# A graph layer's front reordered, its values V split over two row halves, and its z products made of 64 rows

## The chip, the core and the metric

The kernel runs on one core of a Trainium2 chip. The metric is the device time of one execution in microseconds (us). The core has five engines that each work through their own instructions in program order: TensorE (PE, matmuls into PSUM), VectorE (DVE), ScalarE (ACT), GpSimd (POOL) and SyncE (SP, which here only issues DMAs).

## What is computed

`x` has 6,250 nodes of 128 channels; `src`, `dst` are 206,250 edges sorted by `dst`, self edges among them.

```python
h = jnp.maximum(_layernorm(x, axis=-1), 0.0)
feat = jnp.concatenate([h[dst], h[src] - h[dst]], axis=-1)
out = jax.ops.segment_max(feat @ W.T + b, dst, num_segments=6250)
return x + jnp.where(jnp.isfinite(out), out, 0.0)
```

A message is a part of `dst` plus a row B of `src` (B = h times the second half of W). So the kernel needs, for each node, the largest B row among its sources, and adds the part of the node itself at the end.

## The kernel before

**Names.** Nodes are numbered as 125 groups `l` of Q = 50 chunks `q` for B, and as 128 groups of LD = 49 destinations. Each of 128 partitions holds a window of 1,792 edges (`swin` sources, `dwin` destinations; L393, L394). B lies in SBUF as `Bp` (two fp32r parts, high and rest) and in DRAM as `Bt`.

**The front** (up to about 177 us). VectorE counts where each partition's window begins (L339, L388 to L391), and POOL gathers both windows. VectorE makes chunk numbers `q16` (L515 to L518), destinations clamped to their group `dlc` (L519, from `dlf`, which ScalarE writes at L516) and keys `KA`, `KB` (L520, L521). A loop of 44 compares of the keys with themselves shifted (L543 to L560) finds edges that repeat another's chunk and destination; TensorE sums the compares into the PSUM tile `dup` (`count`, L541), together with the masks `out_` (outside the group) and `selfm` (self edge, L561). Woven into this order by `ln_to` are 29 steps of the layernorm and of B: each scales on ScalarE (L454), turns (L460), splits into high and low parts (L462 to L468), multiplies (L477, L478) and copies out (L481 to L483, L494); every fifth one sends ten chunks to `Bt` and x plus the own part to `XA` (L487, L488, both issued by SP). `after` loads x in five groups of ten chunks, each load held back by a tiny copy. `moments`, `roots` and `scales` make the statistics. After the loop VectorE compacts the repeating edges (L571 to L606), POOL scatters them to DRAM (`Lt`, L607), SP reads them back (L612), and from the lists (L629 to L632) POOL begins 432 gathers of B rows (L77). `turned` transposes q16, dlc and the edges' worth into `TQ`, `TD`, `TV`. Some checks of the input stand last (L650 to L697).

**The main loop** (180 to 769 us). 13 tiles `t` of ten groups each (the last of eight) by 25 pairs `i` of chunks. For each pair, `one_hots` makes z in PSUM (L738: a selecting row of `Sel` times `Vb`) for each chunk of the **next** pair and ScalarE turns it into a one-hot by Relu (L739). TensorE multiplies B by the one-hots (L787, four products into `ps`), and VectorE takes the maximum with `acc2` (L798). Between these, `more_rows` issues the repeating edges' steps (L223, VectorE), 432 in all by pair 293, each group of eight stored to `M`. In tile 0, `self_edges` adds four products per pair; in tiles 1 and 2, ScalarE runs one `dump` (L810) per pair.

**V.** `Vb[t % 2]` holds for tile t an edge's source group per chunk and destination: v on rows 0 to 49, its square on rows 64 to 113, two rows of ones. It is built during tile t-1 by a written-out `plan`: `build` (four VectorE pieces per pair of groups), `mats` (14 products of 28 columns into the PSUM tile `pv`, L189, half of them at a time) and `values` (ScalarE). `values` reads `pv` four times (L198 square, L199 identity, for each of two l) and writes the squares shifted (L201): five instructions. It stands at pair 15 for three fifths of the tile, and at pair 23 for the rest. At pair 15 its instructions come ahead of the next half of `mats` (L715 to L720), which writes `pv`; `pv` has one buffer. In the text below a **burst** is one call of `values` in this loop.

**The end.** When the 432 steps have run (pair 293), POOL gathers 49 rows from `M` (L835), and VectorE joins them with `acc` and `XA` (L846 to L863).

Of the kernel before, what the change touches and what calls it, by code (L numbers as in the profile page):

```python
# [41 lines left out]
ONE = 50  # L42
SQ = 64
WN = 14
# [6 lines left out]
def gnn_kernel(tc, x, src, dst, W, b, out):  # L51
# [4 lines left out]
    assert C == P and Q * L == N and Q <= ONE and P * LD >= N and E >= WIN  # L56
# [5 lines left out]
    GQ = 10  # L62
    LASTD = N - (P - 1) * LD
# [16 lines left out]
    with ExitStack() as ctx:  # L80
# [9 lines left out]
        Sz = dram.tile([2 * Q - 1, P], F16, name="Sz")  # L90
        Sm = dram.tile([2 * Q - 1, P], F16, name="Sm")
# [9 lines left out]
        with ExitStack() as body:  # L101
# [5 lines left out]
            Sel = keep.tile([P, Q, P], F16, name="Sel")  # L107
# [40 lines left out]
            def build(u):  # L148

                o = (u % SLOTS) * SLOT  # L150
                OHQ = hx16[:, o:o + P * NBLK].rearrange("p (q b) -> p q b", b=NBLK)
                o += P * NBLK
                w = WN
                if u == NLP - 1:
                    o, w = SLOTS * SLOT, LD
                OHD = hx16[:, o:o + 2 * w * NBLK].rearrange("p (l w b) -> p l w b", w=w, b=NBLK)
                hots[u] = [OHQ, OHD]
                iw = IW if w == WN else IL

                def over(T, n):  # L160
                    return T[:, 2 * u:2 * u + 2].rearrange("p l (o b) -> p l o b", o=1).to_broadcast([P, 2, n, NBLK])

                def cmp_q(a, z):
                    iq = IQ[:, a:z].rearrange("p (o q) b -> p o q b", o=1).to_broadcast([P, 2, z - a, NBLK])
                    oh = at(OHQ, a * NBLK, [list(OHQ.ap[0]), [SQ * NBLK, 2], [NBLK, z - a], [1, NBLK]])
# [9 lines left out]
                return [cmp_d, mul_d, lambda: cmp_q(0, 25), lambda: cmp_q(25, Q)]  # L175
# [16 lines left out]
            def values(t, a, z):  # L192

                z = min(z, cols[t] // (2 * LD))
                pv, v, f = (m[:, :cols[t]].rearrange("q (p l d) -> q l p d", l=2, d=LD) for m in (pvs[t], Vb[t % 2], Vsq))
                for l in range(2):
                    r = slice(SQ * l, SQ * l + Q)
                    A_.activation(f[SQ:SQ + Q, l, a:z], pv[r, l, a:z], AF.Square, bias=shift_c[r, 1:2])  # L198
                    A_.activation(v[:Q, l, a:z], pv[r, l, a:z], AF.Identity, bias=shift_c[r, 0:1])  # L199
                w = slice(a * 2 * LD, z * 2 * LD)  # L200
                A_.activation(Vb[t % 2][SQ:SQ + Q, w], Vsq[SQ:SQ + Q, w], AF.Identity, bias=shift_c[SQ:SQ + Q, 2:3])  # L201

# [36 lines left out]
            with ExitStack() as pre:  # L239
# [64 lines left out]
                for i, v in enumerate((-0.5 * LD - 0.5, -0.25 * (LD * LD - 1), float(-L))):  # L304
                    G_.memset(shifts[:, i:i + 1], v)
# [10 lines left out]

                V.tensor_tensor(crow[:, 0], crow[:, 0], crow[:, 0], ALU.mult)
                V.tensor_scalar(crow[:, 0], crow[:, 0], -1.0, 1.0, op0=ALU.mult, op1=ALU.add)
                V.tensor_scalar(crow[:, 1], crow[:, 0], -2047.0, -2048.0, op0=ALU.is_lt, op1=ALU.mult)
                V.tensor_tensor(rows_[:, 3], crow[:, 0], crow[:, 1], ALU.subtract)  # L320
                V.tensor_copy(rows_[:, 2], crow[:, 1])
# [46 lines left out]
                brow = pool.tile([P, 2 * C], F32R, name="brow")  # L368
# [10 lines left out]
                for r in (0, 32):  # L379
                    V.memset(bsel[r:r + 1].bitcast(F32), 1.0)  # L380
                    A_.copy(brow[r:r + 1, C:], bsrc[r:r + 1])
                V.tensor_tensor(wlo, wT, whi.bitcast(F32), ALU.subtract)
                V.tensor_tensor(brow[32:33, C:], bsrc[32:33], brow[32:33, C:].bitcast(F32), ALU.subtract)
# [3 lines left out]
                after(V, blk_f[:1], GQ)  # L387
# [10 lines left out]


# [23 lines left out]
                for T, i in ((Sz, 0), (Sm, 1)):  # L423
                    for q0 in (0, Q):
                        nc.sync.dma_start(T[q0:q0 + Q - 1], zero[:Q - 1, :P].bitcast(F16))
                    nc.sync.dma_start(T[Q - 1:Q], rows_[:, i])
                nc.sync.dma_start(at(So, 0, [[2 * P, 1], [1, 2 * P]]), rows_[:, 2:4])

                for T, k0 in ((Sz, 0), (Sm, SQ)):
                    nc.sync.dma_start(selv[k0:k0 + Q], at(T, 0, [[P, Q], [1, Q * P]]))  # L430
                    nc.sync.dma_start(selv[k0 + Q:k0 + SQ], at(Sz, 0, [[0, SQ - Q], [0, Q], [1, P]]))
                nc.sync.dma_start(selv[ONE:ONE + 2], at(So, 0, [[P, 2], [0, Q], [1, P]]))
                nc.sync.dma_start(M_v[:, 0], none)

# [5 lines left out]
                V.memset(lw[96:], 0.0)  # L440
# [29 lines left out]
                def ln_mul(k):  # L470
                    st = steps[k]
                    st["pm"] = ps_m.tile([P, 2, 2 * C], F32, name="pm")
                    for j in range(2):
                        o = st["pm"][:L, j]
                        hi, lo = (slot(i, k)[:, j, :L] for i in (1, 2))
                        for a, w in ((bsel, brow), (hi, whi), (hi, wlo), (lo, whi), (lo, wlo)):
                            T_.matmul(o, a, w, start=j == 0 and a is bsel, stop=True, skip_group_check=True)  # L477
                    T_.matmul(st["pm"][:L, :, C:], ident[:L, :L], xs[:, 2 * k:2 * k + 2], start=False, stop=True,  # L478
                              skip_group_check=True)
# [28 lines left out]
                dlf = dwin.bitcast(F32)  # L508
                dlc = pool.tile([P, WIN], BF16, name="dlc")
                selfm = KB[:, :WIN].bitcast(BF16)  # L510
                v16 = lists[:, :WIN // 2].bitcast(BF16)
                q16 = pool.tile([P, WIN], BF16, name="q16")
                out_ = TV.rearrange("p s b -> p (s b)")
                ln_to(4)
                V.tensor_scalar(big, swin, (1 - Q) * 0.5, 1.0 / Q, op0=ALU.add, op1=ALU.mult)  # L515
                A_.activation(dlf, dwin, AF.Identity, bias=nthr)  # L516
                V.tensor_scalar(v16, big, MAGIC, -MAGIC, op0=ALU.add, op1=ALU.add)
                V.scalar_tensor_tensor(q16, v16, float(-Q), swin, op0=ALU.mult, op1=ALU.add)  # L518
                V.tensor_scalar(dlc, dlf, 0.0, float(LD + 1), op0=ALU.max, op1=ALU.min)  # L519
                V.scalar_tensor_tensor(KA[:, 64:], dlc, 64.0, q16, op0=ALU.mult, op1=ALU.add)  # L520
                V.tensor_copy(KB[:, 64:], KA[:, 63:63 + WIN])  # L521
                ln_to(6)

                A_.activation(out_, dlc, AF.Square, bias=shifts[:, 0:1])
                A_.activation(out_, out_, AF.Relu, bias=shifts[:, 1:2])
                A_.activation(big, swin, AF.Identity, bias=1.0)
# [16 lines left out]
                for s in range(1, POS + 1):  # L543
                    e = eqs[s % 3]
                    if s in (12, 24):
                        turned(*((q16, TQ) if s == 12 else (dlc, TD)))
# [6 lines left out]
                    count(identb, e, first=s == 1)  # L553
                    for g, s0 in ((2, 8), (3, 14), (4, 20)):
# [5 lines left out]
                    ln_to(6 + 9 * s // POS)  # L560
                V.scalar_tensor_tensor(selfm, dlf, nthr, swin, op0=ALU.subtract, op1=ALU.is_equal)  # L561
                count(nidb, out_)
                count(nidb, selfm, last=True)
# [16 lines left out]
                ln_to(ln_steps)  # L580
                where_i = pool.tile([P, 1], I32, name="where_i")
# [32 lines left out]

                val = q16
# [5 lines left out]
                for v in Vb:  # L621
                    G_.memset(v[96:], 0.0)
                    G_.memset(v[32:64], 1.0)

                for i in range(SLOTS):
                    for o in (Q, SQ + Q):
                        V.memset(hx16[:, i * SLOT + o * NBLK:i * SLOT + (o + SQ - Q) * NBLK], 0.0)
# [21 lines left out]
                same, junk = KA[:, :WIN].bitcast(BF16), KB[:, :WIN].bitcast(BF16)  # L649
                V.tensor_tensor(same[:, 1:], dlc[:, 1:], dlc[:, :WIN - 1], ALU.not_equal)  # L650
                V.tensor_tensor(same[:, 1:], same[:, 1:], selfm[:, :WIN - 1], ALU.mult)
                V.tensor_scalar(same[:, :1], dlc[:, WIN - 1:], float(LD), None, op0=ALU.is_le)
                V.tensor_tensor(same[:, :1], same[:, :1], selfm[:, WIN - 1:], ALU.mult)
                A_.activation(same, same, AF.Copy, accum_out=badc[:, 8:9])

                V.scalar_tensor_tensor(junk[:, 1:], dlf[:, 1:], 1.0, dlf[:, :WIN - 1], op0=ALU.mult, op1=ALU.is_lt,
# [35 lines left out]
                V.tensor_scalar(fl[:, 1:2], dlc[:, :1], 1.0, None, op0=ALU.is_lt)  # L692
                V.tensor_tensor(fl[:, :1], fl[:, :1], fl[:, 1:2], ALU.add)
# [4 lines left out]
            with ExitStack() as main:  # L698
# [33 lines left out]
                def one_hots(t, i):  # L732
                    n = cols[t]
                    both = []
                    for j in range(2):
                        z = ps_z.tile([P, 512], F32, name="z")
                        oh = ohp.tile([L + 1, TL * LD], F32R, name="oh")
                        T_.matmul(z[:, :n], Sel[:, Q - 1 - i - j], Vb[t % 2][:, :n], start=True, stop=True)  # L738
                        A_.activation(oh[:, :n], z[:L + 1, :n], AF.Relu)  # L739
                        both.append(oh)  # L740
                    return both
# [34 lines left out]
                for k, (t, i) in enumerate(pairs):  # L776
# [8 lines left out]
                    for j in range(2):  # L785
                        for e in range(2):
                            T_.matmul(ps[:, j, :n], Bp[:, e, i + j], oh[j][:, :n], start=e == 0, stop=e == 1)  # L787
# [151 lines left out]
```

## Time and profile before

| | us |
|---|---|
| median of 3 runs (811.27 to 813.49) | 811.47 |
| the profiled execution's own time | 809.35 |
| its span, first to last instruction | 807.6 |
| VectorE busy | 734.2 |
| TensorE busy | 662.4 |
| ScalarE busy | 511.8 |
| POOL busy | 502.5 |
| mean granted TensorE clock (share) | 0.942 |

The page gives busy time by engine, a strip of the span in 40 slices, DMA queues, the chain of work that ended last, and groups of instructions by line with the mean length of one and the idle time before them. A timeline lists instructions with start and length; in square brackets stands the idle time before one and what ended it. Matmuls overlap in the pipeline, so their distance in starts, not their length, is what one costs.

### The profile page before, as it was taken

What the parts mean: (1) busy time and instruction counts of PE and PEld (TensorE: products, weight loads), DVE (VectorE), ACT (ScalarE), POOL (GpSimd) and SP (SyncE); (2) the same over time, 40 slices, a digit from 0 to 9 for tenths busy, and PEclk for the clock granted to TensorE, in tenths of its full rate; (3) what the DMA queues carried; (4) which work ended last, traced back from release to release, by engine and by line L of the source; (5) the groups of instructions that cost most, each with busy time, mean ns of one, the idle gap of its engine ahead of it and who ended that gap; (6) DMA issues with size and microseconds to landing.
All of it is one profiled execution on the core that took longest, in us unless ns stands there. A gap on an engine that the chain in (4) does not pass through costs nothing.

```text
span 807.6 us, 12060 instructions
## 1 busy us (share of the span) xinstructions
PE 662.4 (82%) x3646; PEld 434.2 (54%) x3646; DVE 734.2 (91%) x1368; ACT 511.8 (63%) x1130; POOL 502.5 (62%) x538
## 2 busy tenths in 40 slices
PE   1688977259898998799989998989989999989950
PEld 0455766138765565455555555555555555556730
DVE  6698899888789899999999999999999999998972
ACT  2664487046789999667575766666576666657800
POOL 5200000377777777777777777777777777774773
PEclk9999999559999899799999999999999999999975
DMA  4631222312333333333333373333343333334152
GB/s 126 178 106 46 64 65 71 99 47 79 93 87 105 102 105 101 106 104 102 102 102 105 101 190 106 101 103 103 107 114 105 108 105 103 102 104 124 54 161 84
DMA packets 79650, 82.09 MB, mean 102 GB/s; under 512 B 11699, under 2 KB 68503, under 8 KB 79223
## 3 DMA queue, kind: packets, MB, share of 16 engines
q1 hardware_dynamic: 63038, 46.54, 20.4%
q0 software_dynamic: 15840, 33.93, 14.8%
q10 hardware_dynamic: 700, 0.78, 0.5%
q8 instruction: 30, 0.49, 0.2%
q14 instruction: 42, 0.34, 0.1%
HBM read 42.34 MB, written 38.82 MB: 100 GB/s over the span
## 4 chain that ended last, share of the span: by engine, by line
DVE 41%; PE 23%; issue 17%; ACT 10%; DMA 5%; POOL 2%; DVEq 0%; POOLq 0%; SPq 0%; ACTq 0%
DVE acc L798 16%; PE ps L787 10%; DVE rows L223 9%; ACT oh L739 4%; PE z L738 4%; PE dup L541 3%; DVE acc L593 3%; DMA rows<-Bt,lists 3%; PE pv L189 2%; DMA rows<-M,last_e 2%; ACT dump L810 2%; POOL rows L77 1%; ACT Vb L199 1%; ACT Vsq L198 1%; DVE acc L592 1%
## 5 line engine op out<-in xcount | busy, mean ns | idle before, releaser
L77 POOL DMA_INDIRECT rows<-Bt,lists x432 | 437.2, 1012 | 137.4 <-DMA rows<-Bt,lists 44.5
L739 ACT ACTIVATE oh<-z 126x490 fp32r<-126x490 f32 (+1 forms) x650 | 336.7, 574 | 156.7 <-PE z L738 149.6
L787 PE MATMUL ps<-oh,Bp 126*128 126x490 f32 (+1 forms) x1300 | 390.2, 423 | 23.4 <-DVE acc L798 16.2
L798 DVE TENSOR_TENSOR acc<-acc,ps 128x980 f32<-128x980 f32 (+1 forms) x312 | 359.2, 1151 | 23.4 <-PE ps L787 19.7
L787 PEld LDWEIGHTS ps<-oh,Bp 126*128 126x128 f32 x1300 | 235.3, 193 | 147.5 <-DVE acc L798 90.7
L738 PE MATMUL z<-Vb,Sel 128*128 128x490 f16 (+1 forms) x650 | 194.7, 378 | 14.7 <-ACT oh L739 8.8
L223 DVE SCALAR_TENSOR_TENSOR rows<-rows,lists 128x128 f32<-128x128 f32 x431 | 148.0, 343 | 1.4 <-DMA rows<-Bt,lists 0.4
L189 PEld LDWEIGHTS <-HX 128*128 128x128 bf16 x896 | 68.3, 159 | 52.7 <-issue 37.3
L189 PE MATMUL pv<-HX 128*128 128x28 bf16 (+1 forms) x826 | 74.0, 232 | 16.2 <-ACT Vb L199 16.2
L607 POOL DMA_INDIRECT Lt<-big,where_i x1 | 1.0, 1037 | 120.4 <-DVE big L606 120.4
L738 PEld LDWEIGHTS <-Sel 128*128 128x128 f16 x650 | 43.1, 104 | 55.5 <-issue 53.9
L166 DVE TENSOR_TENSOR HX<-T,IQ 128x700 bf16<-128x700 bf16 x128 | 65.5, 515 | 0.0
L77 POOL DMA_INDIRECT rows<-M,last_e x40 | 38.2, 956 | 12.2 <-issue 7.0
L541 PE MATMUL dup<-rows,identb 128*128 128x512 bf16 (+1 forms) x176 | 36.7, 352 | 4.4 <-DVE rows L552 3.9
L810 ACT ACTIVATE dump<-lists,nbias 128x512 bf16<-128x512 f32 x50 | 37.0, 741 | 0.1
L541 PEld LDWEIGHTS <-identb 128*128 128x128 bf16 x176 | 17.0, 97 | 21.2 <-issue 6.1
L552 DVE TENSOR_TENSOR rows<-KA,KB 128x1792 bf16<-128x1792 int16 x22 | 23.8, 1082 | 3.7 <-PE dup L541 3.7
L477 PE MATMUL pm<-whi,lhl 128*125 128x256 f32 x100 | 26.6, 287 | 0.0
L477 PE MATMUL pm<-wlo,lhl 128*125 128x256 f32 x100 | 26.5, 287 | 0.0
L552 DVE TENSOR_TENSOR rows<-KA 128x1792 bf16<-128x1792 int16 x21 | 22.8, 1085 | 1.4 <-PE dup L541 1.4
L454 ACT ACTIVATE rows<-HX,nmr,rstd 125x128 f32<-125x128 f32 x50 | 22.8, 525 | 1.1 <-DVE rows L440 1.1
L173 DVE TENSOR_TENSOR HX<-HX,T 128x392 bf16<-128x392 bf16 x64 | 23.2, 363 | 0.3
(239 smaller groups left out, 564.4 us busy)
## 6 DMA issues: line engine op xcount, KB each, us to landing
M<-rows SPq DMA_DIRECT2D x54, 512.0 KB
rows<-Bt,lists POOLq DMA_INDIRECT x432
HX<-in_x SPq DMA_DIRECT2D x5, 560.0 KB
Bt<-acc SPq DMA_DIRECT2D x5, 560.0 KB
XA<-HX SPq DMA_DIRECT2D x5, 560.0 KB
out_x<-rows SPq DMA_DIRECT2D x4, 448.0 KB
xa<-XA SPq DMA_DIRECT2D x1, 1512.0 KB
T<-XA SPq DMA_DIRECT2D x1, 1176.0 KB
```

What stands on the lines that cost most here:

```text
L77: G_.indirect_dma_start(out=o, out_offset=None, in_=table, in_offset=bass.IndirectOffsetOnAxis(ap=idx, axis=0))
L166: V.tensor_tensor(oh, over(TQ, z - a), iq, ALU.is_equal)
L189: T_.matmul(o2[:, :, lo:lo + w], OHQ[:, :, i], OHD[:, :, :, i], start=False, stop=True, skip_group_check=True)
L223: V.scalar_tensor_tensor(G[:, j], state["prev"], slim[:, k:k + 1], G[:, j], op0=ALU.min, op1=ALU.max)
L477: T_.matmul(o, a, w, start=j == 0 and a is bsel, stop=True, skip_group_check=True)
L541: T_.matmul(dup[:, c0:c1], m, e[:, c0:c1], start=first, stop=last)
L552: V.tensor_tensor(e, KA[:, 64:], i1, ALU.is_equal)
L738: T_.matmul(z[:, :n], Sel[:, Q - 1 - i - j], Vb[t % 2][:, :n], start=True, stop=True)
L739: A_.activation(oh[:, :n], z[:L + 1, :n], AF.Relu)
L787: T_.matmul(ps[:, j, :n], Bp[:, e, i + j], oh[j][:, :n], start=e == 0, stop=e == 1)
L798: V.tensor_tensor(a, a, ps[:, :, :n], ALU.max)
L810: A_.activation(dump, sdl, AF.Sign, scale=2.0, bias=nbias[:, c:c + 1], accum_out=ends[:, c:c + 1])
```

## The change

- **Clamp.** `dlf` and ScalarE's L516 go; `dlc` is made by two VectorE instructions from the integers. Keys use a factor 128.
- **Layernorm later.** Steps done before the loop and in it: 4 and 6 (before 6 and 9). x's second group is loaded after the window gathers like the others and its statistics move from ahead of the loop into it. `selfm` (now from bfloat16, against a shifted source `sl16` that ScalarE makes) and both mask counts move into the loop; `turned` of q16 and dlc moves behind the layernorm's last step.
- **XA.** One copy of x to XA, DRAM to DRAM, and per group an adding DMA that POOL issues; the product with x (L478) goes, and one of two products with the bias.
- **Checks.** The `same` part moves up to just behind the read of the lists; two tiny instructions go.
- **V** on four 32-row strips: chunks 0 to 24 on rows 0 to 24 with squares on 32 to 56, chunks 25 to 49 on rows 64 to 88 with squares on 96 to 120. `values` becomes ten instructions of the same columns. A pair is now chunk i/2 of each half; z comes from a product of 64 rows on rows 0 to 63 and one on 64 to 127. `Sel` halves.

```diff
                 for l in range(2):
-                    r = slice(SQ * l, SQ * l + Q)
-                    A_.activation(f[SQ:SQ + Q, l, a:z], pv[r, l, a:z], AF.Square, bias=shift_c[r, 1:2])
-                    A_.activation(v[:Q, l, a:z], pv[r, l, a:z], AF.Identity, bias=shift_c[r, 0:1])
+                    for h in range(2):
+                        r, o = (slice(o, o + H) for o in (SQ * l + SH * h, SQ * h))
+                        o2 = slice(SQ * h + SH, SQ * h + SH + H)
+                        A_.activation(f[o2, l, a:z], pv[r, l, a:z], AF.Square, bias=shift_c[r, 1:2])
+                        A_.activation(v[o, l, a:z], pv[r, l, a:z], AF.Identity, bias=shift_c[r, 0:1])
                 w = slice(a * 2 * LD, z * 2 * LD)
-                A_.activation(Vb[t % 2][SQ:SQ + Q, w], Vsq[SQ:SQ + Q, w], AF.Identity, bias=shift_c[SQ:SQ + Q, 2:3])
+                for o in (SH, SQ + SH):
+                    A_.activation(Vb[t % 2][o:o + H, w], Vsq[o:o + H, w], AF.Identity, bias=shift_c[o:o + H, 2:3])
...
-                after(V, blk_f[:1], GQ)
...
-                moments(GQ, 2 * GQ)
-                roots(GQ, 2 * GQ)
-                scales(GQ, 2 * GQ)
-                for q0 in range(2 * GQ, Q, GQ):
+                for q0 in range(GQ, Q, GQ):
                     after(G_, dwin, q0)
...
+                for l0, l1 in ((0, N // P * P), (N // P * P, N)):
+                    o, i = (a[l0:l1].rearrange("(p r) c -> p (r c)", p=min(P, l1 - l0)) for a in (XA, x))
+                    nc.sync.dma_start(o, i)
...
-                            nc.sync.dma_start(XA_l[p0:p1, q0:q0 + GQ], xs[p0:p1, q0:q0 + GQ])
+                            G_.dma_start(XA_l[p0:p1, q0:q0 + GQ], xs[p0:p1, q0:q0 + GQ], accum_op=ALU.add)
...
-                V.tensor_scalar(dlc, dlf, 0.0, float(LD + 1), op0=ALU.max, op1=ALU.min)
-                V.scalar_tensor_tensor(KA[:, 64:], dlc, 64.0, q16, op0=ALU.mult, op1=ALU.add)
+                V.tensor_scalar(dlc, dwin, nthr, 0.5, op0=ALU.add, op1=ALU.max)
+                V.tensor_scalar_min(dlc, dlc, LD + 0.5)
+                V.scalar_tensor_tensor(KA[:, 64:], dlc, 128.0, q16, op0=ALU.mult, op1=ALU.add)
...
+                    if s == 6:
+                        count(nidb, out_)
+                    if s == 9:
+                        V.tensor_tensor(selfm, dlc, sl16, ALU.is_equal)
+                        count(nidb, selfm)
-                    for g, s0 in ((2, 8), (3, 14), (4, 20)):
+                    for g, s0 in ((1, 1), (2, 9), (3, 17), (4, 25)):
...
-                    ln_to(6 + 9 * s // POS)
+                    ln_to(4 + 6 * s // POS)
...
-                        T_.matmul(z[:, :n], Sel[:, Q - 1 - i - j], Vb[t % 2][:, :n], start=True, stop=True)
+                        r = slice(SQ * j, SQ * (j + 1))
+                        T_.matmul(z[:, :n], Sel[r, H - 1 - i // 2], Vb[t % 2][r, :n], start=True, stop=True)
```

More of the change, by code (lines that the diff above doesn't have):

```diff
@@ L106, in gnn_kernel @@
             Bp = keep.tile([L + 1, 2, Q, C], F32R, name="Bp")
-            Sel = keep.tile([P, Q, P], F16, name="Sel")
+            Sel = keep.tile([P, H, P], F16, name="Sel")
             acc = keep.tile([P, Q * (L + 1)], F32, name="acc")
@@ L367, in gnn_kernel @@
                 bsel = pool.tile([P, L], F32R, name="bsel")
-                brow = pool.tile([P, 2 * C], F32R, name="brow")
+                brow = pool.tile([P, 2, C], F32R, name="brow")
                 whi = pool.tile([P, 2 * C], F32R, name="whi")
@@ L580, in gnn_kernel @@
                 ln_to(ln_steps)
+                turned(q16, TQ)
+                turned(dlc, TD)
                 where_i = pool.tile([P, 1], I32, name="where_i")
@@ L646, in gnn_kernel @@
                     f()
[L649 to L656, printed above, removed]
+                V.scalar_tensor_tensor(junk[:, 1:], dwin[:, 1:], 1.0, dwin[:, :WIN - 1], op0=ALU.mult, op1=ALU.is_lt,
                                        accum_out=badc[:, 0:1])
```

94 lines of the change are left out of this document (46 added, 48 removed).

## The prediction

> **What bounds the kernel now.** I read the strip of the page first, then busy time tile by tile, then waits in the main loop, then one burst of `values` in the timeline, then VectorE alone in the front.
>
> ```profile
> DVE  6698899888789899999999999999999999998972
> ...
> L798 DVE TENSOR_TENSOR acc<-acc,ps 128x980 f32<-128x980 f32 (+1 forms) x312 | 359.2, 1151 | 23.4 <-PE ps L787 19.7
> ...
> L738 PE MATMUL z<-Vb,Sel 128*128 128x490 f16 (+1 forms) x650 | 194.7, 378 | 14.7 <-ACT oh L739 8.8
> ```
>
> VectorE is full from the second slice almost to the end. By tile (start to start of a tile's first maximum; columns PE, PEld, DVE, ACT, POOL):
>
> ```profile
> 426.89:471.89 45.00, 41.83 (x224) 25.00 (x224) 44.85 (x85) 30.07 (x60) 34.64 (x35) 1.00 0.44 123
> ```
>
> This is tile 5: VectorE has 44.85 of 45.00 us, 1.80 per pair. It is the bound of tiles 3 to 10, and what TensorE saves there buys nothing by itself. TensorE's own need, from distances of starts (two z 0.43, four products 1.00, and 7 products of `mats` 0.42 twice in five pairs), is 1.60 per pair: 0.20 of slack. Where VectorE does wait, it waits once or twice a tile:
>
> ```profile
> DVE acc L798 <- PE ps L787: 19.7, 23, 3.2
> ...
> PE pv L189 <- ACT Vb L199: 16.2, 12, 2.1
> ```
>
> (Waits between 180 and 740 us: total, times, longest.) Twelve waits of TensorE for the last read of `pv`: one for each burst at pair 15. That of tile 5:
>
> ```profile
> 449.90 0.38 ACT L198 ACTIVATE Vsq<-pv,shift_c 50x147 f32<-50x147 f32 x1
> ...
> 450.29 0.38 ACT L199 ACTIVATE Vb<-pv,shift_c 50x147 f16<-50x147 f32 x1
> ...
> 450.69 0.38 ACT L198 ACTIVATE Vsq<-pv,shift_c 50x147 f32<-50x147 f32 x1
> ...
> 451.09 0.38 ACT L199 ACTIVATE Vb<-pv,shift_c 50x147 f16<-50x147 f32 x1
> 451.50 0.54 ACT L201 ACTIVATE Vb<-Vsq,shift_c 50x294 f16<-50x294 f32 x1
> 451.52 0.57 PE L189 MATMUL pv<-HX 128*128 128x28 bf16 x7 [0.98 <-ACT Vb L199]
> ...
> 451.93 0.58 PE L738 MATMUL z<-Vb,Sel 128*128 128x490 f16 x2
> 452.17 1.24 PE L787 MATMUL ps<-oh,Bp 126*128 126x490 f32 x4
> ...
> 453.44 1.18 DVE L798 TENSOR_TENSOR acc<-acc,ps 128x980 f32<-128x980 f32 x1
> ```
>
> Four reads, 0.40 apart; TensorE stands 0.98 until the last is done, then runs `mats`, z and the products that VectorE needs. They end at 453.40; VectorE had been free since 453.39. **The slack here is zero**, and in none of the twelve tiles is there more.
>
> The front, VectorE alone:
>
> ```profile
> 33.54 1.09 DVE L519 TENSOR_SCALAR dlc<-dwin 128x1792 bf16<-128x1792 f32 x1 [5.81 <-ACT dwin L516]
> ...
> 37.39 1.09 DVE L552 TENSOR_TENSOR rows<-KA,KB 128x1792 bf16<-128x1792 int16 x1
> ...
> 101.63 2.02 DVE L571 TENSOR_SCALAR KA<-dup 128x1792 bf16<-128x1792 f32 x1 [0.86 <-PE dup L541]
> ```
>
> It waits 5.81 for ScalarE's clamp; it is nearly full afterwards.
>
> **The front, step by step.**
> 1. *To the first compare.* Five small crow instructions and the copy at L268 leave the way to the window's begin: 0.5. x's second group (0.64 MB) no longer moves ahead of the window gathers (1.84 MB): the DMA ran at 330 GB/s there, so the gathers take 5.6 from about 16.7, plus 0.8 to the semaphore: dst at 23.1 (before 24.86), src about 20.3. From there VectorE runs L515, L517, L518 (1.13, 1.13, 2.05), the clamp (1.1, and 0.6 as L521), L520 2.05, L521 0.65: first compare at 29.0, not 37.39. **-8.4.**
> 2. *The loop.* It took 59.4: 44 compares at 1.00, three groups of moments at 3.1, and 5.85 of waits for TensorE. Now 44.1, four groups 12.4, selfm 1.05: 57.6. TensorE needs 44 x 0.75, 1.5 for the masks and 6 x 1.9: 46, so it no longer holds VectorE. The new moments wait for x's second group: its tiny POOL copies squeeze between VectorE's instructions (one took 2.00 beside L518), issue about 25.8, landed 3.4 later as the third group did: 29.2, needed at 30.0. If it is late, 1 to 2 us.
> 3. *After the loop.* L561 (2.06) and the wait of 0.86 before L571 are gone. L571 at 29.0 + 57.6 + 2.05 = 88.7, not 101.6: **-13.**
> 4. *Layernorm later.* 16 steps, not 11, stand before the product that VectorE needs at L596. A step took 3.01 there: 0.93 of ScalarE copies, 0.06, L492 0.22, ten products at 0.12, L478 0.63 to the release. With nine products and no L478 it would be 2.46; ScalarE's own work in it is 2.49. So 87.4 + 1.9 + 15 x 2.5 = 127; VectorE comes at 88.7 + 40.25 = 128.9. Hidden, by 2 us.
> 5. *Scatter and read back.* L606 ends at 135.4 (-12.9), but on POOL the last adding DMAs are queued ahead of the scatter; they wait for a copy at 134.7. No row shows an adding DMA. Bounds: issue as a gather (0.95 + 0.30 each; scatter at 137.3), or data at a tenth of the 330 GB/s (0.64 MB, 19 us, partly ahead of the scatter's own data). Nearest is the plain XA store of the same bytes, which lands in a few us: I take 3 lost. L629 at 145.5, not 154.96: -9.5 (-2 to -12).
> 6. *Checks* after L632 lose `same` and two small ones: 2.75, which run while VectorE waits for the lists. **Front: -12.2** (-5 to -15).
>
> ScalarE's extra instructions in the two first `values` (+4) end before the checks do (168.3 against 176.95, both moved): hidden.
>
> **The main loop.** VectorE's work is unchanged. The change adds five ScalarE instructions to each burst; their length goes with the columns (147, 98), not with the rows, so each costs the same again.
> - *Pair 15:* eight reads of `pv`, not four: TensorE waits 4 x 0.40 longer with nothing behind it that could run, and VectorE loses all of it: 12 x 1.6 = **+19.2**. The next one-hots come 2.1 later, still in time for the shifted pair 16.
> - *Pair 23:* five more cost 4 x 0.36 + 0.46 = 1.9. Queued behind them on ScalarE are the one-hots of pair 24, for which L787 waits (467.30 in tile 5). The products end at 468.53, VectorE comes at 469.56: slack 1.0 in tiles 3 to 6, 0.6 to 0.75 in 7 to 10, none in 0 to 2. So 4 x 0.9 + 4 x 1.25 + 3 x 1.9 = **+14.5**; that of tile 11 falls behind pair 293, where POOL's gathers from M bound the end.
> - *Tiles 1 and 2*, where ScalarE has 45.7 of 48.2, pay the whole 4.05 per tile: +1.
> - *z.* No product of 64 rows is in this trace. Floor: the two run at once, one of 0.215 saved per pair. Ceiling: they don't, and TensorE empties before and after: a z takes 0.378 but starts are 0.212 apart (tail 0.17, as much for the products after it), and the weight loads of 0.104 and 0.193 show: +0.6. Overlapped but emptied is +0.39. I take the middle of -0.215 and +0.39, +0.09, which lies under the slack of 0.20: 0 (-3 to +7, since the burst at pair 23 eats the same slack).
>
> The Trainium skill, TensorEngine Tiling (Array Packing), Key Properties, speaks on both sides: row tiles can work in parallel, and changing the tiling mode drains TensorE. No run here shows either; by the first alone z costs -0.2 per pair and the sum is the same, by the second it is the second rival.
>
> **Sum:** 809.35 - 12.2 + 19.2 + 14.5 + 1 = 831.9 against the profiled execution; the median shown is 2.1 above that one, so **834**. This case's own range: 822 to 848.
>
> **Rivals.**
> - *A faster kernel:* TensorE is what feeds the bursts, and with z nearly free it would have caught up enough for 1.6 and 1.9 to vanish. Then only the front counts: 811.5 - 12 = 799. For it: tile 0 is partly TensorE's. Against: at pair 15 TensorE stands still for ScalarE, and no speed of its own helps. It decides if the reads of `pv` in a burst take no longer than 1.7 us together.
> - *TensorE becomes the bound:* each pair goes from 128 rows to 64 and back. From a net +0.20 per pair on, every pair of tiles 1 to 11 pays: at +0.29, 0.09 x 275 = 25, tile 0 another 7, and the burst at pair 23 loses its slack (8 x 0.9 = 7): 873; at +0.39, 900. For it: two exposed weight loads and two tails are real durations. Against: at least one of the two z should overlap.
> - *The front gives nothing:* adding DMAs or a late x group eat the 12: 846.
> - *Half a burst:* bursts cost half of what I say, front at its best: 811, no change.
>
> **Chances.** Forecast 0.55, TensorE-bound 0.18, front lost 0.12, faster 0.12, half bursts 0.03. Leaving out the faster and half cases and the upper end of the TensorE-bound one: 812 to 880. 0.3% (2.4 us) is about what a measurement of this kernel can tell from none: faster 0.12, same 0.03, slower 0.85.
>
> **What would show it.** In the profile after: first L552-like compare near 29 us and lists near 145.5; the wait of `mats` for the last L199-like read about 2.6 in place of 0.98, with VectorE idle 1.6 before pair 15's maximum; tiles 4 to 6 near 47.5 us, not 45.1. I am wrong if the tiles keep 45, or if VectorE waits for TensorE in every pair.

## The result: slower, 880.7 us

The changed kernel takes 880.74 us in the median (875.22 to 884.45) beside 811.73 of the kernel before on the same chip: 1.084 times as long [1.079, 1.090]; such ratios and their intervals are taken from each kernel's fast executions alone. The forecast was 834, range 812 to 880. Slower was right, and the two mechanisms named are there, but the time is 47 us above the forecast and just outside the range.

In the page of the changed kernel (span 873.5 us) VectorE's row in the strip is no longer full, and in the group of its maxima (L800 now) the idle time ahead has gone from 23.4 to 95.9 us, while the busy time stands. The z products (L739 now) cost TensorE less, 140.9 in place of 194.7.

```profile
DVE  4999997786697977989888898878979888894883
...
PEclk9999997598798988989989899878989988996995
...
L800 DVE TENSOR_TENSOR acc<-acc,ps 128x980 f32<-128x980 f32 (+1 forms) x312 | 359.9, 1153 | 95.9 <-PE ps L789 94.6
...
L739 PE MATMUL z<-Vb,Sel 64*128 64x490 f16 (+1 forms) x650 | 140.9, 409 | 36.1 <-ACT Vb L205 23.3
```

Three sums locate the 65.9 us by which the span grew from 807.6. The first maximum comes at 170.62, not 180.07: -9.45. From there to the maximum of pair 293 (L800 in tile 11, pair 17; "the loop" below) it takes 625.5, not 550.3: **+75.3**. Behind it, +0.1. The loop stretch in busy time by window, first the kernel before, then the changed one (length, busy time of PE, PEld, DVE, ACT and POOL, mean granted TensorE clock, DMA share, GB/s):

```profile
180.07:730.32 550.25, 502.64 (x2683) 318.92 (x2683) 528.99 (x982) 391.42 (x825) 419.10 (x417) 0.97 0.38 105
```

```profile
170.62:796.14 625.52, 541.46 (x2684) 330.91 (x2683) 532.29 (x981) 435.48 (x940) 415.21 (x417) 0.88 0.35 92
```

VectorE's work is the same (529.0 and 532.3). ScalarE has 44 us more. The column to notice is the clock: 0.97 has become 0.88. The trace's record of the granted clock has 27.9 us at one half in the loop before and 148.1 after, in pieces of 3.4, 6.8 and 10.2 us, nearly all of them from pairs 14 and 23 on, which is where the bursts are (4.0 and 4.7 us of the two sums are the end of one long piece that began in the front). The burst at pair 15 of tile 5, in the timeline (columns: start, length, engine, line):

```profile
471.68 0.38 ACT L201 ACTIVATE Vsq<-pv,shift_c 25x147 f32<-25x147 f32 x1
...
474.43 0.38 ACT L202 ACTIVATE Vb<-pv,shift_c 25x147 f16<-25x147 f32 x1
...
474.83 1.10 ACT L205 ACTIVATE Vb<-Vsq,shift_c 25x294 f16<-25x294 f32 x2
474.86 0.56 PE L190 MATMUL pv<-HX 128*128 128x28 bf16 x7 [2.62 <-DVE HX L171]
...
475.35 0.38 PE L739 MATMUL z<-Vb,Sel 64*128 64x490 f16 x2
...
475.66 2.00 PE L789 MATMUL ps<-oh,Bp 126*128 126x490 f32 x4
...
477.69 1.17 DVE L800 TENSOR_TENSOR acc<-acc,ps 128x980 f32<-128x980 f32 x1 [2.60 <-PE ps L789]
```

Eight reads 0.39 apart; `mats` waits 2.62 for the last of them (the line names L171, which ended at 474.82, and the last read ended at 474.81; in eight of the twelve tiles the line names the read): the 0.98 of before plus 1.6, as forecast. The next line is the surprise: the four products take **2.00**, where they took 1.24 before. From 475.7 the clock is at one half for 3.4 us. VectorE waits 2.60 where the forecast had 1.6.

The burst at pair 23 of the same tile. Its Relus of pair 24 come behind it, z waits 1.98 for V and then for a buffer that those Relus free, the products run at half clock again, and VectorE waits 2.35:

```profile
489.56 0.34 ACT L201 ACTIVATE Vsq<-pv,shift_c 25x98 f32<-25x98 f32 x1
...
492.38 0.94 ACT L205 ACTIVATE Vb<-Vsq,shift_c 25x196 f16<-25x196 f32 x2
492.89 0.57 PE L739 MATMUL z<-Vb,Sel 64*128 64x490 f16 x1 [1.98 <-ACT Vb L205]
493.34 1.99 ACT L742 ACTIVATE oh<-z 126x490 fp32r<-126x490 f32 x4
493.97 0.57 PE L739 MATMUL z<-Vb,Sel 64*128 64x490 f16 x1 [0.51 <-ACT oh L742]
494.47 2.00 PE L789 MATMUL ps<-oh,Bp 126*128 126x490 f32 x4
...
496.51 1.17 DVE L800 TENSOR_TENSOR acc<-acc,ps 128x980 f32<-128x980 f32 x1 [2.35 <-PE ps L789]
```

All in all VectorE's waits ahead of the maxima of pairs 15 to 17 rose from 10.8 to 46.6 us in the loop, and of pairs 24, 0, 1 and 2 (the first three pairs of tile 0 left out) from 3.9 to 38.9: +70.8 of the 75.3. Pairs away from bursts are as before: the median step from one maximum to the next is the same at every pair from 6 to 14, 1.35 to 2.04 us.

### The profile page after: what moved, and what is told of

Read it like the earlier page. It is cut to its first block, busy times and chain, and to the rows that moved or that the text cites. A ratio compares the mean times of both kernels' runs of the same rounds, so it can differ in the third digit from the quotient of the medians.

```text
span 873.5 us, 12053 instructions
## 1 busy us (share of the span) xinstructions
PE 698.1 (80%) x3566; PEld 435.1 (50%) x3571; DVE 732.7 (84%) x1374; ACT 560.7 (64%) x1260; POOL 510.2 (58%) x548
## 4 chain that ended last, share of the span: by engine, by line
PE 35%; DVE 29%; ACT 13%; issue 13%; DMA 4%; POOL 1%; DVEq 0%; POOLq 0%; SPq 0%; ACTq 0%
PE ps L789 22%; DVE acc L800 10%; PE z L739 7%; DVE rows L227 6%; ACT oh L742 4%; PE pv L190 3%; ACT Vb L202 3%; ACT Vsq L201 3%; DVE rows L551 3%; DVE acc L596 3%; DMA rows<-Bt,lists 2%; ACT dump L812 1%; PE z L749 1%; DVE acc L595 1%; ACT Vb L205 1%
## 5 line engine op out<-in xcount | busy, mean ns | idle before, releaser
L742 ACT ACTIVATE oh<-z 126x490 fp32r<-126x490 f32 (+1 forms) x650 | 336.9, 575 | 185.6 <-PE z L739 184.4
L800 DVE TENSOR_TENSOR acc<-acc,ps 128x980 f32<-128x980 f32 (+1 forms) x312 | 359.9, 1153 | 95.9 <-PE ps L789 94.6
L789 PE MATMUL ps<-oh,Bp 126*128 126x490 f32 (+1 forms) x1300 | 413.7, 445 | 18.7 <-DVE acc L800 15.8
L789 PEld LDWEIGHTS ps<-oh,Bp 126*128 126x128 f32 x1300 | 245.3, 210 | 145.5 <-DVE acc L800 54.0
L739 PE MATMUL z<-Vb,Sel 64*128 64x490 f16 (+1 forms) x650 | 140.9, 409 | 36.1 <-ACT Vb L205 23.3
L739 PEld LDWEIGHTS <-Sel 64*128 64x128 f16 x650 | 32.6, 94 | 103.1 <-issue 94.0
L490 POOL DMA_DIRECT2D XA<-HX x10 | 9.8, 1212 | 96.4 <-ACT lhl L472 75.9
L78 POOL DMA_INDIRECT rows<-M,last_e x40 | 38.4, 959 | 12.2 <-issue 7.9
L78 POOL DMA_INDIRECT HX<-M,last_e x9 | 8.5, 944 | 50.2 <-DMA M<-rows 47.8
L202 ACT ACTIVATE Vb<-pv,shift_c 25x147 f16<-25x147 f32 (+2 forms) x96 | 34.1, 355 | 1.8
L201 ACT ACTIVATE Vsq<-pv,shift_c 25x147 f32<-25x147 f32 (+2 forms) x96 | 34.0, 354 | 1.3
L496 ACT CAST Bp<-pm 125x256 fp32r<-125x256 f32 x25 | 9.7, 387 | 35.1 <-PE pm L494 35.1
L205 ACT ACTIVATE Vb<-Vsq,shift_c 25x294 f16<-25x294 f32 (+2 forms) x52 | 25.6, 493 | 1.3
```

Of the source, the lines that this page charges most:

```text
L78: G_.indirect_dma_start(out=o, out_offset=None, in_=table, in_offset=bass.IndirectOffsetOnAxis(ap=idx, axis=0))
L201: A_.activation(f[o2, l, a:z], pv[r, l, a:z], AF.Square, bias=shift_c[r, 1:2])
L202: A_.activation(v[o, l, a:z], pv[r, l, a:z], AF.Identity, bias=shift_c[r, 0:1])
L739: T_.matmul(z[:, :n], Sel[r, H - 1 - i // 2], Vb[t % 2][r, :n], start=True, stop=True)
L789: T_.matmul(ps[:, j, :n], Bp[:, e, i // 2 + H * j], oh[j][:, :n], start=e == 0, stop=e == 1)
L800: V.tensor_tensor(a, a, ps[:, :, :n], ALU.max)
```

## The experiments

Theory A: a burst is longer than what one pair leaves free on ScalarE, TensorE and VectorE wait for it, and TensorE then runs on at half its clock. C: the length alone, at an unchanged clock (the forecast). B: 64-row products among 128-row ones cost the time. D, in one run: ScalarE's added work in all.

All times with the kernel before on the same chip at 812 to 813 us. "15" and "24": VectorE's waits before the maxima of pairs 15 to 17, and of 24, 0, 1, 2 (without the first three pairs of tile 0), in the loop; "half": the loop's time at half clock. The last four columns are of one execution each, the profiled one. In half bursts the ratio is of five of its ten executions, whose median is 821.4.

| kernel | median us | against before | loop | 15 | 24 | half |
|---|---|---|---|---|---|---|
| before | 811.7 | | 550.3 | 10.8 | 3.9 | 27.9 |
| changed | 880.7 | 1.084 [1.079, 1.090] | 625.5 | 46.6 | 38.9 | 148.1 |
| front only | 803.3 | 0.988 [0.984, 0.992] | 554.3 | 12.8 | 1.9 | 25.7 |
| values twice, 128 rows | 862.5 | 1.060 [1.056, 1.064] | 605.2 | 45.0 | 24.5 | 99.6 |
| half bursts, 64 rows | 825.9 | 1.008 [1.005, 1.011] | 572.9 | 20.3 | 6.4 | 84.3 |
| changed, filled | 839.7 | 1.035 [1.032, 1.038] | 583.2 | 28.9 | 19.1 | 5.0 |
| changed, bursts cut | 836.0 | 1.030 [1.026, 1.034] | 582.7 | 11.2 | 30.1 | 87.0 |
| changed, first burst moved | 897.7 | 1.106 [1.102, 1.110] | 643.5 | 1.6 | 53.2 | 182.5 |
| front only, bursts cut | 802.8 | 0.987 [0.984, 0.990] | 552.1 | 0.7 | 3.6 | 15.1 |

The table leaves out eleven runs, on chips where the kernel before itself took 1124 to 1137 us in the median (1092 to 1161 in single executions) and engines waited up to 29 us at a time for something that the trace does not name; they stand at the end of this section.

**Front only.** The diff of the front, with `values`, `one_hots` and the selector loads of before.

> The front of the changed kernel with V and z of the kernel before. All theories: 802 us (800 to 804) where the kernel before takes 811.7, by the first maximum that falls 9.45 us earlier. Against the run that also cuts the bursts (802.8): the same within 1.5 us if the stream of gathers sets the pace as soon as the bursts stop doing so, over 805 if cutting them had been worth the 10 us expected of it.

803.26 us, as expected: the front is worth 9.3 us (6.7 to 12.7 by the interval). In the profiled execution the first maximum comes 9.4 earlier, but the loop is 4.1 longer than before (554.3). POOL's gathers, which must be through before the maximum of pair 293, begin 7.0 earlier (150.4, before 157.4) and end only 5.7 earlier (721.5, before 727.2).

**Values twice**, in the kernel before:

```
                 for l in range(2):
                     r = slice(SQ * l, SQ * l + Q)
-                    A_.activation(f[SQ:SQ + Q, l, a:z], pv[r, l, a:z], AF.Square, bias=shift_c[r, 1:2])
+                    for _ in range(2):
+                        A_.activation(f[SQ:SQ + Q, l, a:z], pv[r, l, a:z], AF.Square, bias=shift_c[r, 1:2])
...
```

(and the same for the two other instructions, whose lines are left out here.)

> The kernel before with every instruction of values issued twice (the same results written again): 128-row products throughout, bursts of ten instructions in place of five. Theory A/C (burst length): 811.7 plus nearly all of the 75 us that the main loop lost, 877 to 887 us. Rival B (64-row products among 128-row ones cost it): 812.

862.48. Rival B's 812 is out: bursts of ten instructions cost 50 us without one 64-row product. But theory A's 877 is missed too: 20 us of the loop's 75 are not there, 14 of them at pairs 24 to 2.

**Half bursts**, in the changed kernel: `for h in range(1)` and `for o in (SH,)` in `values`, so that rows 64 to 127 of V are never written and the output lacks the values of chunks 25 to 49.

> The changed kernel without the second half of V (never written, so the output lacks the values of chunks 25 to 49): 64-row products as changed, bursts of five instructions. Theory A/C: 802 to 808 us. Rival B: over 865.

825.94: neither. Bursts of five at 64 rows take away most of the loss, yet 19 us more of loop than front only has is left. In the profiled execution 14 of them lie in tile 0, here by window (half bursts, then front only): 67.19 in place of 53.21, with a mean clock of 0.73. The first burst is followed by one piece of half clock of 34.1 us there. The ten executions spread more than those of the other kernels of the table, 814 to 834 us, and the longer ones have the lower mean clock (0.93 down to 0.89).

```profile
171.13:238.32 67.19, 65.13 (x323) 49.50 (x322) 46.61 (x81) 40.26 (x87) 50.33 (x54) 0.73 0.30 84
```

```profile
170.70:223.91 53.21, 49.74 (x326) 42.25 (x326) 45.91 (x81) 39.46 (x88) 40.44 (x42) 0.98 0.33 92
```

**Filled**, in the changed kernel:

```
+                    fill = i // 2 in (15, 24)
+                    if fill:
+                        ps = ps_s.tile([P, 2, 512], F32, name="ps")
+                        for _ in range(8):
+                            T_.matmul(ps[:, 0], Bp[:, 0, 0], Bp[:, 0, 0:4], start=True, stop=True)
                     for f in plan.get((t, i // 2), ()):
                         f()
...
```

> The changed kernel with eight more 512-column products on TensorE at pairs 15 and 24, ahead of the one-hot products; bursts as they are; the results of the added products are overwritten. Theory A (the halved clock behind each burst is what the forecast left out, some 40 us): 835 to 850 us. Theory C (the length of the bursts on ScalarE is all of it, the halved clock only goes with it): 870 to 890 us, though the half clock goes from behind the bursts.

839.74 us, in theory A's range, and the run that decides: 64-row products and bursts as they were, more work on TensorE, and 41 us less. The loop has 5.0 us at half clock in place of 148.1, and the clock column says 1.00:

```profile
172.32:755.56 583.24, 536.43 (x2868) 336.28 (x2867) 529.25 (x981) 435.36 (x940) 416.34 (x417) 1.00 0.36 99
```

The same burst of tile 5 in its timeline (L787 are the added products, L795 the pair's own, L806 the maxima):

```profile
455.36 2.11 PE L787 MATMUL ps<-Bp 126*128 126x512 f32 x8 [0.63 <-DVE acc L806]
...
457.33 1.10 ACT L205 ACTIVATE Vb<-Vsq,shift_c 25x294 f16<-25x294 f32 x2
457.36 0.58 PE L190 MATMUL pv<-HX 128*128 128x28 bf16 x7
...
458.18 1.15 PE L795 MATMUL ps<-oh,Bp 126*128 126x490 f32 x4
...
459.37 1.18 DVE L806 TENSOR_TENSOR acc<-acc,ps 128x980 f32<-128x980 f32 x1 [1.79 <-PE ps L795]
```

The burst takes as long as before; the products behind it take 1.15, not 2.00, and VectorE waits 1.79, not 2.60. What is left is what the forecast had: +33.0 in the loop (forecast 34.7), +18.0 at pairs 15 to 17 (19.2), +15.1 at pairs 24 to 2 (15.5 with tiles 1 and 2). The fit is closer than the comparison can bear: the kernel before, from which these are counted, has 27.9 us of half clock itself, and the added products take time too.

**Bursts cut.** `values` gets as arguments which of the two l to do and whether to write the squares, and is called in pieces of at most six instructions; the second half of `mats` for the tile's last pair of groups comes one pair earlier.

```
-                    at_pair(t, 5 * r + 2, lambda u=u: mats(u, NBLK // 2, NBLK, (ps_v, "pv")))
+                    at_pair(t, 5 * r + 2 - (r == PL - 1), lambda u=u: mats(u, NBLK // 2, NBLK, (ps_v, "pv")))
                     if r == 2:
-                        at_pair(t, 15, lambda t=t: values(t + 1, 0, 3))
+                        for i, how in ((13, ((0,), False)), (14, ((1,), False)), (16, ((), True))):
+                            at_pair(t, i, lambda t=t, how=how: values(t + 1, 0, 3, *how))
                     if u == NLP - 1 or r == PL - 1:
-                        at_pair(t, 5 * r + 3, lambda t=t: values(t + 1, 3, PL))
+                        for i, how in ((0, ((0,), False)), (1, ((1,), True))):
+                            at_pair(t, 5 * r + 3 - (r == PL - 1) + i, lambda t=t, how=how: values(t + 1, 3, PL, *how))
```

> The changed kernel, its halves of V and 64-row products kept, but each burst of values cut into pieces of four reads or fewer in different pairs (13, 14 and 16 in place of 15; 22 and 23 in place of 23, with the last one-hot products one pair earlier). Theory A/C (a burst stalls because it is longer than what one pair leaves free on ScalarE): the 75 us that the main loop lost come back nearly whole, 800 to 815 us where the kernel before takes 811.7, and the interval to pair 15's maximum falls from 4.3 to 4.9 us to 2.3 or less. Rival B (64-row products among 128-row ones): 865 and more, intervals as in the changed kernel. Rival D (ScalarE's added work in all, about 96 us of a main loop of 590, is what the loop pays): 860 and more, the idle time only moved to other pairs.

835.96. Rival D is out: ScalarE's added work is all still there (435.7 us busy in the loop, as in the changed kernel's 435.5), and 43 of the loop's 75 us are back. Not "nearly whole": the first burst, in pieces of four, costs no more than before the change (11.2 against 10.8), but the second, whose last piece has six, still stalls pair 24 (30.1), with a piece of half clock of 6.8 us behind it in most tiles.

**First burst moved**, whole, `values(t + 1, 0, 3)` from pair 15 to 18, behind the products of `mats` ("one-hot products" in the expectation) of pairs 15 and 17.

> The changed kernel with its first burst (ten instructions, uncut) moved from pair 15 to pair 18, behind the one-hot products of pairs 15 and 17, so that these no longer wait for it. If the loss at pair 15 needs the one-hot products queued behind the burst: the stall of pair 15 goes and none comes at pair 18, 840 to 850 us. If the burst's length on ScalarE is enough by itself (it delays the two Relus behind it): the stall of 2.6 us comes back at pair 19, 870 to 885 us.

897.70, above both ranges: the stall goes from pair 15 (1.6 us left) and comes at pairs 18 to 20 (47.0; in the changed kernel 1.0), no smaller, and half clock grows to 182.5 us. In tile 5, in the timeline (L739 z, L742 its Relu):

```profile
487.07 0.38 ACT L201 ACTIVATE Vsq<-pv,shift_c 25x147 f32<-25x147 f32 x1
...
490.23 1.10 ACT L205 ACTIVATE Vb<-Vsq,shift_c 25x294 f16<-25x294 f32 x2
...
491.35 1.99 ACT L742 ACTIVATE oh<-z 126x490 fp32r<-126x490 f32 x4
491.99 0.56 PE L739 MATMUL z<-Vb,Sel 64*128 64x490 f16 x1 [3.05 <-ACT oh L742]
...
492.48 2.00 PE L789 MATMUL ps<-oh,Bp 126*128 126x490 f32 x4
...
494.52 1.17 DVE L800 TENSOR_TENSOR acc<-acc,ps 128x980 f32<-128x980 f32 x1 [3.02 <-PE ps L789]
```

No product of `mats` waits here. The Relus stand behind the burst in ScalarE's order, the next z needs a buffer that they free, and VectorE waits 3.02, with the products at 2.00 once more. So the length of the burst is enough by itself; it is not the wait for `pv` in particular.

**Front only, bursts cut**: the best of both, since a burst of five at 128 rows also stalled pair 15.

> The front of the changed kernel, V and z of the kernel before, and the bursts of values cut over several pairs as in the run that cuts them in the changed kernel. Where the kernel before takes 811.7: 802 from the front alone, less the 10.9 us that VectorE waits at pairs 15 to 17 and part of the 3.9 at pairs 24 to 2: 790 to 800 us. If bursts of five instructions cost nothing that cutting recovers: 802.

802.78, 1.3% below the kernel before, but not below front only (803.26, on another chip): the 790 to 800 hoped for were missed, and the 802 of the expectation's other branch came for a reason that it does not name. The waits at pair 15 are gone, 0.7 in place of 12.8. In their place stands another (waits of 180 to 740 us: total, times, longest):

```profile
DVE rows L224 <- DMA rows<-Bt,lists: 12.4, 21, 1.9
```

That was 0.4, once, before (4.2 in front only). VectorE's stream step now waits for POOL's gathers: 432 of them at 1.0 us each with 0.3 between run from the lists on almost without a gap, and the last one ends at 721.0. In front only (721.5) and in the kernel before (727.2) they run just as densely, with one gap of over 1 us each, so the gathers set the pace as soon as the bursts do not, and cutting bursts has little left to win.

**Runs on disturbed chips.** Front only, values twice, half bursts and filled were first tried there, in this order:

> The change's front with the V, the z products of 128 rows and the five-instruction bursts of before. If the front gained what the two traces show between them at the first maximum (180.07 against 170.62), 811.7 - 9.5 = 802 us, and tiles 4 to 6 at 45 us each. If instead the new front disturbs the main loop (adding DMAs, gathers that begin earlier), tiles of 47 us or more and a time above 811.

> The kernel before with every instruction of values issued twice (the second writes the same values again): V, z of 128 rows and the front stay. Theory A (the length of a burst, and the halved clock that TensorE gets after standing still for it): nearly the whole loss of the main loop, 811.7 + 65 to 75 = 877 to 887 us, VectorE idle 2.5 to 3 before the maximum of pair 15. Theory C (the length of a burst at an unchanged clock, my forecast's sizes): 811.7 + 35 = 846, idle 1.6. Theory B (the change between 64 and 128 rows costs TensorE): no change, 812.

> The changed kernel with the second half of V never written (rows 64 to 127 keep the 1.0 of their memset), so that a burst is five instructions again; the z products of 64 rows stay. Chunks 25 to 49 give wrong one-hots, the instructions that follow are the same. Theories A and C: the loop is that of before, 802 us, up to 808 where the products of 64 rows use up slack. Theory B: above 865, tiles still 50 us or more.

> The changed kernel with eight filler products of 126 rows and 512 columns (overwritten by the real ones) ahead of the plan's work of pairs 15 and 24 of every tile, so that TensorE is not idle while ScalarE works off a burst. Theory A: the clock stays at 1.0 through the bursts, and VectorE's idle falls to the 1.6 and about 1 per tile of the lengths alone: 835 to 850 us. Theories B and C: nothing to win from activity, 875 to 890.

1130.6, 1141.0, 1142.6 and 1157.5 us, beside 1137.2 of the kernel before: no theory's numbers. Again, on another chip:

> The front of the changed kernel with V and z of the kernel before. Its first maximum falls 9.45 us earlier in the trace of the changed kernel; nothing behind it is touched. All theories: 811.7 - 9.45 = 802 us (800 to 804), and no more half clock than before (24 us). If it is at 811, what the front gains is given back at the end.

> The kernel before, with every instruction of values issued twice (the same results are written again): 128-row products throughout, eight reads and two spreads for each part of a tile instead of four and one. Theory A (a longer burst makes TensorE stand still for the one-hots, and it then runs at half clock): 811.7 plus most of the 75 us that the main loop lost, 877 to 887 us, with over 100 us at half clock. Rival C (longer bursts at an unchanged clock, as forecast): 846. Rival B (the change between 64-row and 128-row products): 812.

> The changed kernel without the second half of V (it is never written, so the output lacks the values of chunks 25 to 49): bursts of four reads and one spread, as before the change; 64-row products as changed. Theories A and C (burst length): 802 to 808 us, half clock back to some 25 us. Rival B (64-row products among 128-row ones): over 865.

> The changed kernel with eight more 512-column products on TensorE at pairs 15 and 24, ahead of the one-hot products, so that it has work while it waits for the values' burst; the bursts stay as they are, and the results of the added products are overwritten. Theory A (the halved clock is what the forecast left out): most of the 136 us at half clock goes, 835 to 850 us. Rivals B and C (the clock follows something else): 875 to 890, since the added products take some 1 us each time.

1120.9, 1143.9, 1127.3 and 1141.1 us, beside 1124.5. And front only on a third:

> The front of the changed kernel with V and z of the kernel before. Its first maximum falls 9.45 us earlier in the trace of the changed kernel, and nothing behind it is touched. All theories: 811.7 - 9.45 = 802 us (800 to 804), and no more half clock than before (24 us). If it is at 811, what the front gains is given back at the end.

1142.9 us, beside 1127.4. Nothing can be said from these sums. Two details of the traces agree with the later runs: front only's first maximum at 170.4, 170.2 and 171.0 us; and half clock in the 9 us from the first read of a burst, summed over the 24 bursts, 118 and 116 us with values twice and 51 and 34 in the filled runs. Over the whole loop, though, half clock is about as long in both there (343 and 345 us, 336 and 328). Two last runs, bursts cut and filled, and values twice and filled, were to settle whether the 20 us between the changed kernel and values twice are the clock's:

> The changed kernel with its bursts cut over several pairs and added products on TensorE (four at pair 15, six at pair 24) that keep its clock up; the results of the added products are overwritten. With both causes gone, only the 64-row products are left of the change behind the front. If they cost the loop only through the clock: the loop to pair 293's maximum takes some 570 us (552 of the run that cuts the bursts at 128 rows, and some 15 of waiting that is left at pair 24), 815 to 824 us in all. If they cost by themselves, 830 or more.

> The kernel before with every instruction of values issued twice and eight added products on TensorE at pairs 15 and 24 (their results are overwritten): the bursts of the change at 128 rows and with the clock kept up, beside the filled run of the changed kernel (64 rows, loop 583.2 us). If the row tiling costs only through the clock: the same loop of 580 to 586 us, 842 to 850 us in all. If 64-row products cost the loop 20 us by themselves: a loop of 563, 825 us.

1164.7 and 1159.3 us, beside 1137.0: they fell on such a chip too, and that stays open.

## Why the prediction missed

- **Front, -12.2: right in kind, 2.75 too large.** VectorE alone, changed kernel:

```profile
25.89 1.15 DVE L517 TENSOR_SCALAR dlc<-dwin,nthr 128x1792 bf16<-128x1792 int32 x1
...
30.46 1.09 DVE L551 TENSOR_TENSOR rows<-KA,KB 128x1792 bf16<-128x1792 int16 x1
...
90.55 2.02 DVE L572 TENSOR_SCALAR KA<-dup 128x1792 bf16<-128x1792 f32 x1
...
130.94 0.16 DVE L599 TENSOR_SCALAR S<-dup 128x1 f32<-128x1 f32 x1
...
147.70 0.61 DVE L638 TENSOR_TENSOR big<-big,KA 128x432 f32<-128x432 f32 x1 [3.89 <-DMA KA<-Lt]
```

  The wait of 5.81 for ScalarE's clamp is gone, and VectorE clamps in 1.15 and 0.63. The first compare came at 30.46, not 29.0 (src landed at 21.7, not 20.3; its gather was issued at 16.21, which is 0.3 later than before and not 0.5 earlier); L572, L571 of before, at 90.55, not 88.7; S0 at 130.94, not 128.9, with layernorm hidden as argued; the lists' step at 147.70, not 145.5. The 3 us for the adding DMAs were about right, though not where I put them: the last two hold POOL until 138.27, but the scatter starts only 1.2 behind its data (0.8 before); it is the read back that comes later, issued 5.95 after the scatter's start (2.88 before). From the scatter's data to the lists it took 10.3 us, 3.7 more than before. The checks shrank by 2.2, not 2.75. Two of the prediction's additions are slightly off and do not matter: -12.9 and 3 give -9.9, not -9.5, and the three products at pair 23 give 14.3, not 14.5.
- **Pair 15, +19.2, and pair 23, +14.5: the steps that failed.** Measured, they are +35.8 and +35.0. Their mechanism stands: eight reads, a wait of 2.62, the one-hots behind five more instructions. With the clock kept up they are +18.0 and +15.1, and the filled run's whole differs from the sum by 5.5 only: 4.4 of front (its first maximum came 7.8 earlier, not 12.2), 2.7 behind the loop, -1.7 in it. What the terms left out is that TensorE does what follows a burst at half clock: 42.3 us (625.5 - 583.2), more than the two terms together. The sum took 1.24 for the products behind the wait, the duration that the profile showed behind a wait of 0.98. The warning stood in the trace of before: tile 0's mean clock of 0.93, and 3.4 us pieces of half clock from pair 14 of tiles 0 to 2 and pair 23 of tiles 1 and 2 on, behind waits of TensorE of 1.1 to 2.1 us. I read the clock as a mean (0.942), not by place.
- **z, net +0.09 per pair, hidden:** the two now start 3 ns apart, before 212. Where TensorE alone sets the pace a pair went from 1.32 to 1.40: +0.08 (in tile 12, 1.08 to 1.18). That the middle of two bounds came so near is luck, since no row decided between them. Most of the first bound's gain is eaten by something around the products, and neither shows in the loop: filled, the loop is 28.9 longer than front only's, and the waits at the bursts make up 33.3. The rival that TensorE becomes the bound gave 873 to 900, which holds the measured time, but not by its mechanism: pairs without a burst did not slow.
- **The rivals that ended faster or at no change** needed TensorE to catch up, or bursts at half the forecast price; the bursts cost twice that price.
- **Open in part: 64-row products and the clock.** With bursts of the same length, 64-row products go with more half clock than 128-row ones: 148.1 against 99.6 us (loop 20.4 us longer), and at bursts of five 84.3 against 25.7 (18.6 longer). The traces of the table show where it comes from. In their loops the clock's record changes only on a fixed grid of 3.41 us. At bursts of ten, full clock gives way to half about as often, 24 times at 64 rows and 22 at 128, but half clock stays on for a further stretch 18 times against 6. In the four loops with 128-row products it stayed on only after stretches in which TensorE was busy (as the window view counts it) for 0.59 to 0.81 of the time, and ended whenever that share was 0.85 or more; in the changed kernel it stayed on after 6 stretches with a share of 1.00. So at equal busy time, 64-row products do less to bring full clock back. That whatever grants the clock counts rows or work, and not time, fits this; it is argued, not shown.

The Trainium skill, "TensorE: Matmul & The Clock Gate", Part 1, says that TensorE falls to half clock after about one idle window of 3.4 us and comes back after a busy one. The quantum agrees with this record: 3.4, 6.8, 10.2. The condition does not, read as one gap of that length: half clock came after waits of 2.62 us, and in tiles 0 to 2 of the kernel before after waits of 1.1 to 2.1.

## What to carry to other kernels

Ask of each added wait of an engine in a tight chain not only how long it is but at what speed the engine comes back: price the work behind the wait at half clock as well, and read the granted clock by place, not as a mean. An instruction burst on a helper engine is free only up to what one step leaves over and should be cut over several steps before it grows past that: here five instructions of 0.4 at once already cost 10.8 us of waits, one or two at a time 0.7. Moving a burst whole only moves the stall. When a stall is taken away, look for the stream just below it, here the gathers, before counting the gain.

## What the runs showed of the hardware

- Half clock followed waits of TensorE of 1.1 to 2.1 us in the kernel before and of 1.7 to 3.8 us in the changed one, and eight added products of 512 columns (2.11 us, put into the wait) kept it away: 148.1 us of half clock became 5.0, and a kernel with more work ran 41 us faster.
- The clock changed only on a grid of 3.41 us. With 128-row products half clock stayed on only after stretches in which TensorE was busy for at most 0.81 of the time; with 64-row products it stayed on after stretches with a share of 1.00 too.
- A us of half clock cost 0.30 us of this loop (42.3 for 143.1), the time of the added products not counted.
- ScalarE's reads of 25 rows take what those of 50 took, 0.377 and 0.382 us at 147 columns: halving the rows halves nothing.
- Two products of 64 rows on different row halves start 3 ns apart, and still a pair that TensorE paces got 0.08 us longer.
- The last two adding DMAs held POOL 1.67 us together.
